# The last two chunks' routing dealt one and two steps later, with a norm, the last scaled values and the copy of turned weights moved

## The chip, the cores and the metric

The kernel runs on one core of a Trainium2 chip. The metric is the time of one execution on the device in microseconds (us), the median of several runs. A core has five engines with an instruction queue each: TensorE (PE in the profile), VectorE (DVE), ScalarE (ACT), GpSimd (POOL), and SyncE (SP), which issues most of the transfers here. An instruction waits for its semaphores at the head of its engine's queue, so that everything behind it on that engine waits too.

## The reference

The input is 32 sequences of 256 tokens with 128 features. The part that matters, shortened:

```python
h = layernorm(x) * (1 + ca) + sa
x = x + ga * attention(h)          # 16 heads of 64; softmax over the QUERY axis
h = layernorm(x) * (1 + cb) + sb
x = x + gb * moe(h)

# moe(h): 32 experts in 4 groups, 2 groups kept for each token, 6 experts of those
scores = sigmoid(h @ gate_weight.T); sc = scores + gate_bias
group_scores = top_k(sc.reshape(T, 4, 8), 2)[0].sum(-1)     # the 2 best groups are kept
topidx = top_k(where(kept, sc, -inf), 6)                    # the 6 best experts
tw = scores[topidx] / sum * 0.2
routed = sum over those experts of tw * (silu(h @ w_gate) * (h @ w_up)) @ w_down
shared = silu(h @ shared_w_gate) * (h @ shared_w_up) @ shared_w_down
anchor = one expert of 16, picked by topidx[:, 0], with weight 0.1
return routed + shared + 0.1 * anchor
```

## The kernel before

**Stages.** The tokens are cut into 16 chunks of 512. The attention stage has 128 steps (8 for each chunk, each with two heads of two sequences), numbered s, and three more in which the pipeline runs empty (to s = 130). Then come 7 steps (131 to 137) of the shared expert, each for a pair of chunks. Then come 35 lists of up to 512 gathered rows, all of one group of experts. A list j has five units k = 0 to 4, written (j, k) here.

**A step of attention.** `score_products(s)` on PE, `lowest` on DVE and `exponential` on ACT make the exponentials with their sums. `inverse_sums(s - 1)` (L568, DVE) and `scaled_values(s - 1)` (L579, POOL) divide the values by those sums into the tile `vs`. `weighted_sums(s - 2)` (L597, PE, tile `pav`) needs `vs`, and `project` (L479, tile `po`) follows.

**Portions.** The norms before and after attention and the routing are cut into portions. A table gives for each the step, relative to the first of its chunk, and the place in the step (TOP, PROD, MID, END); `deal(s, where)` issues them there. The order on each engine is the order of the program's text. From step 138 on a step is two units of a list, with TOP and PROD behind the products of the first of them and MID and END behind those of the second:

```python
if step <= last:
    half = (j * (KU + 1) + k) % 2
    for where in ((TOP, PROD), (MID, END))[half]:
        deal(step, where)
    step += half
```

The portions that matter here, for chunk c: `norm2_normalize` (L359 to L384, POOL, at 14 END), `norm2_modulate` (L394, POOL, 15 END), `norm2_send` (SP, 16 END: to DRAM and back in another order, tiles `hd_ln` and `hb_ln`), `norm2_turn` (L664, DVE, 19 TOP), `route_logits` (L479, tile `pl`, PE, and L685 `th`, ACT, 19 PROD), `route_mask` (23 TOP), `route_counts` (L762, POOL, tile `cnt`, 23 END), `route_top` (L814 and L815, memsets on POOL, then L817 to L819 on DVE, 23 MID), `route_ranks` (L479, tile `pr`, PE, 24 PROD), `route_weights` (25 TOP), `route_place` (L791 to L803, DVE, with L802, tile `to`, on POOL, 26 TOP), `route_write` (26 END) and eight `route_send` (L865, POOL, tile `rows`, 27 to 30 END). Chunk 14 begins with step 112 and chunk 15 with step 120, so that their routing falls into the shared pairs and the first lists.

**A unit of a list.** `up(j, k)` issues the products `pg` and `pu` (L1252, PE), the silu (L1256, ACT) and two products on DVE, with `pu` (L1257) and with the spread weights `bt` (L1258). Then `down` of the unit before follows (L1280, PE, tile `py`). With the first unit of list j comes `send(j - 1)`: ACT copies `py` to `y` (L1288), and POOL issues four indirect transfers of `y` to DRAM (L1291). At k = 0 SP issues the loads of the rows of list j + 3 and of the weights of list j + 2. At k = 2 `weights_turn(j + 2)` transposes the routing weights on PE (L1220, tile `pc`), copies them on ACT (L1222, tile `cwt`) and sends them to DRAM (L1224, tile `cd`); at k = 4 `weights_spread(j + 2)` loads them, repeated over the partitions (L1234, tile `bt`). At k = 1 and 3 `split_weights` (L1203 and L1207, ACT) rearranges the weights of list j + 1, and at k = 3 `rows_turn` (L1242, DVE) turns its rows.

Of the kernel before, what the change touches and what calls it, by code (L numbers as in the profile page):

```python
# [29 lines left out]
NCH = B * S // CH  # L30
# [10 lines left out]
LISTS = 2 * B * S // CH + NG - 1  # L41
# [17 lines left out]
def adaln_block_kernel(  # L59
# [23 lines left out]
    nc = tc.nc  # L83
# [155 lines left out]
    with tc.tile_pool(name="mod", bufs=1) as mp, tc.tile_pool(  # L239
# [13 lines left out]
        for b in range(BPC):  # L253
            nc.tensor.matmul(
                pmb[:, b].rearrange("p j d -> p (j d)"), silb[:, b, :], wmod_sb[:, 0 : 2 * D],
                start=True, stop=True,
# [70 lines left out]
    NS = NCH * NP  # L327
# [3 lines left out]
    with ExitStack() as actx:  # L331
# [241 lines left out]
        def scaled_values(s):  # L573
            c, t = divmod(s, NP)
            vt, rc = step_of["v", s // HALF], step_of.pop(("rc", s))
            vs = vsp.tile([P, BPC * 2, 2, DH], F32, tag="vs", name=f"vs_{s}")
            col = (t % HALF) * P
            for b in range(BPC):
                nc.gpsimd.tensor_tensor(  # L579
                    vs[:, 2 * b : 2 * b + 2],  # L580
                    vt[:, 2 * b : 2 * b + 2, col : col + P].rearrange(
                        "p k (h d) -> p k h d", h=2
                    ),
                    rc[:, b].unsqueeze(3).to_broadcast([P, 2, 2, DH]),
                    ALU.mult,
                )
            step_of["vs", s] = vs
# [295 lines left out]
        TOP, PROD, MID, END = range(4)  # L883
# [188 lines left out]

        portions = {}

        soon = {-6: 0, -5: 0, -4: 0, -3: 0, -2: 1, -1: 1, 0: 2, 1: 2}
        for c in range(NCH):
            for at, where, portion in table[0 if c else NORM1 :]:
                if c == 1 and portion is load_x:
                    continue
                if c == 1:  # L1080
                    at = soon.get(at + NP, at + NP) - NP
                portions.setdefault(c * NP + at, []).append((where, portion, c))

        def deal(s, where):
            for w, portion, c in portions.get(s, []):
                if w == where:
                    portion(c)
# [71 lines left out]
        T = [{} for _ in range(LISTS)]  # L1159
# [53 lines left out]
        def weights_turn(j):  # L1213

            t = T[j]
            rw = t.pop("rw")
            t["ix"] = mp.tile([P, NT], U32, tag="ix", name=f"iy_{j}", bufs=5)
            nc.vector.tensor_copy(t["ix"], rw[:, :, GW - 1])
            pc = ps_mm.tile([NT * OWN, P], F32, tag="mm", name=f"pc_{j}")
            nc.tensor.transpose(pc, rw.rearrange("p i w -> p (i w)"), ident)  # L1220
            cwt = mp.tile([NT * OWN, P], F32, tag="cwt", name=f"cwt_{j}", bufs=2)
            nc.scalar.copy(cwt, pc)  # L1222
            cd = cwd.tile([OWN, CH], F32, tag="cd", name=f"cd_{j}")
            nc.sync.dma_start(out=cd.rearrange("w (i p) -> i w p", p=P), in_=cwt)  # L1224
            t["cd"] = cd

        def weights_spread(j):

            t = T[j]
            cd = t.pop("cd")  # L1230
            bt = bcp.tile([P, 2, CH], F32, tag="bt", name=f"bt_{j}")
            for n, part in enumerate((cd[0:EPG], cd[EPG : GW - 1])):
                of = part.shape[0]
                nc.sync.dma_start(  # L1234
                    out=bt[:, n, :], in_=part.unsqueeze(0).to_broadcast([P // of, of, CH])
                )
            t["bt"] = bt

        def rows_turn(j):
            t = T[j]  # L1240
            t["h"] = mp.tile([P, CH], F32, tag="h", name=f"h_{j}", bufs=2)
            nc.vector.transpose(t["h"], t.pop("rh").rearrange("p x r -> p (x r)"))  # L1242
# [61 lines left out]
        def shared_up(n):  # L1304
            cs = 2 * n, 2 * n + 1
            pg, pu = (ps_sc.tile([P, CH], F32, tag="sc", name=f"{k}_{n}") for k in ("sg", "su"))
            for ps, w in ((pg, sg_sb), (pu, su_sb)):
                for h, c in enumerate(cs):
                    nc.tensor.matmul(  # L1309
                        ps[h * SI : (h + 1) * SI], w, h2_all[c], start=True, stop=True  # L1310
                    )
            a = hid.tile([P, CH], F32, tag="a", name=f"sa_{n}")
            nc.scalar.activation(a, pg, AF.Silu)
            nc.vector.tensor_mul(a, a, pu)  # L1314
            return n, a

        def shared_down(n, a, banks):
            cs = 2 * n, 2 * n + 1
            py = [
                p.tile([P, NT, D], F32, tag=tag, name=f"sy_{c}")  # L1320
                for c, (p, tag) in zip(cs, banks)
            ]
            for i in range(NT):
                for h in range(2):
                    nc.tensor.matmul(  # L1325
                        py[h][:, i, :],
                        a[h * SI : (h + 1) * SI, i * P : (i + 1) * P],
                        sd_sb[h * SI : (h + 1) * SI],
                        start=True,
                        stop=True,  # L1330
                    )
            for h, c in enumerate(cs):
                if n < PAIRS:
                    (nc.scalar.copy, nc.vector.tensor_copy)[h](
                        h2_all[c], py[h].rearrange("p i d -> p (i d)")
                    )
                    continue

                o = h2_all[c].rearrange("p (i d) -> p i d", d=D)
                for b in range(BPC):  # L1340
                    nc.vector.tensor_tensor(
                        tokens(o)[:, b], tokens(py[h])[:, b], by_batch(S_[c]["gate"])[:, b],
                        ALU.mult,
                    )
                nc.vector.tensor_add(x1_all[c], x1_all[c], o)
# [55 lines left out]
        for n in range(PAIRS):  # L1401
            now = shared_up(n)
            if prev is not None:
                shared_down(*prev, two_banks)
            prev = now
            for where in range(4):
                deal(step, where)
            step += 1
            if n == 2:
                weights_turn(0)  # L1410
            if n == 3:
                weights_turn(1)
                weights_spread(0)
            if n == 4:
                weights_spread(1)
                rows_turn(0)
            if n == 5:
                split_weights(0, "wg")
                split_weights(0, "wu")
# [10 lines left out]
        for j in range(LISTS):  # L1430

            bounds = (0, NT) if j < LISTS - 1 else (0, NT // 2, NT - 1, NT)
            parts = [slice(*p) for p in zip(bounds, bounds[1:])]
            for k, part in ((k, part) for part in parts for k in range(KU + 1)):
                a = up(j, k, part)
                if prev is not None:
                    down(*prev)
                    if prev[1] == KU:
                        send(prev[0], prev[2])
                prev = (j, k, part, a)  # L1440
                if part.start > 0:
                    continue
                if k == 0 and j + 3 < LISTS:
                    fetch_rows(j + 3)
                if k == 0 and j + 2 < LISTS:
                    fetch_weights(j + 2)
                if k == 2 and j + 2 < LISTS:
                    weights_turn(j + 2)
                if k in (1, 3) and j + 1 < LISTS:
                    split_weights(j + 1, ("wg", "wu")[k // 2])  # L1450
                if k == 3 and j + 1 < LISTS:
                    rows_turn(j + 1)
                if k == 4 and j + 2 < LISTS:
                    weights_spread(j + 2)

                if step <= last:
                    half = (j * (KU + 1) + k) % 2
# [3 lines that stand above are left out]
                elif late:  # L1461
                    late.pop(0)()

                if (j, k) in due:
                    due.pop((j, k))()
                if k == 4 and started < NCH and complete[started] <= j:
                    if started == NCH - 2:
                        load_gate(NCH - 1)
                    pass_load(started)
                    at = ((j + 2, 0), (j + 2, 4)) if j < LISTS - 2 else ((j + 1, 2), (j + 1, 4))  # L1470
                    due[at[0]] = lambda c=started: pass_sum(c)
                    due[at[1]] = lambda c=started: pass_out(c)
                    started += 1
# [62 lines left out]
```

## Time and profile before

| | |
|---|---|
| median of 3 runs | 1380.83 us (1380.76 to 1381.69) |
| the profiled execution | 1397.12 us, of which its span is 1395.2 us |
| PE busy | 1342.8 us, 96% of the span |
| DVE, ACT, POOL busy | 73%, 62%, 54% |
| mean granted clock of PE | 0.99 of full speed |
| transfers | 153.32 MB, 110 GB/s in the mean |

The profile shows one execution, which is 16.3 us longer than the median of the timed runs. The view of windows gives the busy time of each engine in stretches of the span, with the granted PE clock; 20.00 under PE in a stretch of 20 us means no pause. In the timeline a row has the start, the duration, engine, line, operation and tiles, and in brackets the idle time of that engine before it with what ended it.

### The profile page before, as it was taken

The page shows a single profiled execution, that of the slowest core. Times are in us where ns is not written, and L with a number is a line of the kernel's source. Part 1 is how long each engine was busy: PE and PEld are TensorE (multiplying, and loading weights), DVE is VectorE, ACT ScalarE, POOL GpSimd, SP SyncE. Part 2 cuts the span into 40 slices and gives each one's busy share as a digit, 9 for nine tenths or more (in the row PEclk, how much of TensorE's full clock was granted, in tenths as well). Part 3 has the DMA queues.
Part 4 walks back from the last instruction along what each step waited for, and adds up shares of the span by engine and source line. Part 5 has one row for each costly group of instructions (what it writes and reads, how often), then busy time and mean ns, then how long its engine had stood idle before and what let it go on. Part 6 is the DMA issues. An engine that isn't in the chain of part 4 may idle for free. (4 is left out here: it accounts for less than half of the span.)

```text
span 1395.2 us, 33821 instructions
## 1 busy us (share of the span) xinstructions
PE 1342.8 (96%) x10443; PEld 833.9 (60%) x10443; DVE 1024.7 (73%) x4266; ACT 868.0 (62%) x2883; POOL 758.9 (54%) x1290
## 2 busy tenths in 40 slices
PE   6999999999999999999999998889999999999995
PEld 2566566666666666556666665455566666666664
DVE  5666788778778778887887776755855557888776
ACT  3778677777777777677777776434444444454442
POOL 2536368668668668668668457444333233344342
PEclk9999999999999999999999999999999999999998
DMA  4765721221221221221221211554545557677752
GB/s 155 259 211 176 247 64 42 59 70 40 60 70 39 60 70 37 62 65 38 67 65 38 51 35 52 131 146 120 132 130 138 134 137 191 191 201 192 194 155 74
DMA packets 270686, 153.32 MB, mean 110 GB/s; under 512 B 171014, under 2 KB 234759, under 8 KB 270508
## 3 DMA queue, kind: packets, MB, share of 16 engines
q1 hardware_dynamic: 258908, 129.70, 34.9%
q0 software_dynamic: 10624, 20.40, 4.1%
q8 instruction: 85, 1.39, 0.4%
q10 hardware_dynamic: 976, 1.06, 0.2%
q14 instruction: 93, 0.76, 0.2%
HBM read 91.27 MB, written 60.61 MB: 109 GB/s over the span
## 5 line engine op out<-in xcount | busy, mean ns | idle before, releaser
L560 ACT ACTIVATE e<-e,mn 128x256 f32<-128x256 f32 (+1 forms) x1024 | 454.2, 446 | 203.6 <-DVE mn L550 163.0
L550 DVE CUSTOM_DVE_ANT_0 e<-psc,mask 128x256 f32<-128x256 f32 (+1 forms) x1024 | 306.8, 346 | 10.0 <-PE pav L597 3.8
L1291 POOL DMA_INDIRECT y_d<-y,iy x140 | 140.5, 1004 | 292.1 <-ACT y L1288 256.1
L579 POOL TENSOR_TENSOR vs<-v,rc 128x256 f32<-128x256 f32 x256 | 151.5, 613 | 228.0 <-DVE rc L568 221.2
L529 PEld LDWEIGHTS psc<-q,k 64*128 64x128 f32 x2048 | 166.2, 187 | 113.4 <-issue 101.6
L1257 DVE TENSOR_TENSOR a<-a,pu 128x512 f32<-128x512 f32 (+2 forms) x185 | 121.6, 657 | 139.3 <-PE pu L1252 57.3
L529 PE MATMUL psc<-q,k 64*128 64x256 f32 (+1 forms) x2048 | 202.1, 336 | 0.0
L597 PE MATMUL pav<-e,vs 128*64 128x256 f32 (+1 forms) x2048 | 195.0, 333 | 6.1 <-POOL vs L579 6.1
L1280 PEld LDWEIGHTS py<-wd_sb,a 128*128 128x128 f32 x1120 | 148.4, 193 | 78.2 <-issue 48.6
L560 ACT ACTIVATION_READ_ACCUMULATOR e<-e,mn 128x1 f32 x1024 | 193.7, 189 | 0.0
L1256 ACT ACTIVATE a<-pg 128x512 f32<-128x512 f32 (+2 forms) x185 | 106.1, 573 | 134.4 <-PE pg L1252 103.7
L1252 PE MATMUL pg<-h,wg 128*128 128x512 f32 (+2 forms) x370 | 182.1, 574 | 0.0
L1252 PE MATMUL pu<-h,wu 128*128 128x512 f32 (+2 forms) x370 | 181.3, 572 | 0.0
L479 PEld LDWEIGHTS po<-wo_sb,z 128*64 128x64 f32 x2048 | 122.4, 139 | 70.9 <-issue 69.7
L597 PEld LDWEIGHTS pav<-e,vs 128*64 128x64 f32 x2048 | 126.9, 136 | 58.9 <-POOL vs L579 6.8
L1280 PE MATMUL py<-wd_sb,a 128*128 x1120 | 151.7, 278 | 9.1 <-DVE a L1258 8.6
L490 DVE TENSOR_TENSOR v<-pv,bv_sb 128x512 f32<-128x512 f32 x128 | 88.4, 691 | 92.7 <-PE pv L479 66.7
L865 POOL DMA_INDIRECT rows_d<-rows,ix x128 | 130.9, 1023 | 37.5 <-issue 34.8
L500 DVE TENSOR_SCALAR q<-pq,negbq 128x512 f32<-128x512 f32 x128 | 96.0, 750 | 65.9 <-PE pq L479 64.3
L479 PE MATMUL pv<-wqkv_sb,n_t 128*64 128x512 f32 x512 | 133.1, 600 | 2.9 <-DVE q L500 2.1
L479 PE MATMUL po<-wo_sb,z 128*64 128x128 f32 x2048 | 135.2, 275 | 0.0
L479 PE MATMUL pq<-n_t,wqkv_sb 128*64 128x512 f32 x512 | 133.9, 601 | 0.7 <-ACT n_t L313 0.7
(239 smaller groups left out, 1829.3 us busy)
## 6 DMA issues: line engine op xcount, KB each, us to landing
rows_d<-blank SPq DMA_DIRECT2D x69, 366.0 KB
bt<-cd SPq DMA_DIRECT2D x70, 256.0 KB
rh<-rows_d SPq DMA_DIRECT2D x140, 64.0 KB
wgr<-in_w_gate_dram SPq DMA_DIRECT2D x35, 256.0 KB
wur<-in_w_up_dram SPq DMA_DIRECT2D x35, 256.0 KB
mb<-mod_dram SPq DMA_DIRECT2D x31, 256.0 KB
hb_ln<-hd_ln SPq DMA_DIRECT2D x124, 64.0 KB
s<-y_d SPq DMA_DIRECT2D x30, 256.0 KB
```

The source lines that it names most:

```text
L479: nc.tensor.matmul(ps[r], a[:, r], b, start=start, stop=stop)
L529: nc.tensor.matmul(pb[h][:, cols], k[r, o + kb * P : o + (kb + 1) * P], q[r, o + kb * P : o + S], start=True, stop=True,)
L550: nc.vector.tensor_tensor_reduce(e[:, cols], ps[:, cols], mask[:, cols], 1.0, 3e38, ALU.add, ALU.min, mn[:, b, kb, h : h + 1],)
L560: nc.scalar.activation(e[:, cols], e[:, cols], AF.Exp, bias=mn[:, b, kb, h : h + 1], scale=-1.0, accum_out=sm[:, b, kb, h : h + 1],)
L579: nc.gpsimd.tensor_tensor(vs[:, 2 * b : 2 * b + 2], vt[:, 2 * b : 2 * b + 2, col : col + P].rearrange("p k (h d) -> p k h d", h=2), rc[:, ...
L597: nc.tensor.matmul(pav[h * DH : (h + 1) * DH, o + kb * P : o + S], vs[:, 2 * b + kb, h, :], e[:, 0 : 2 * P] if kb == 0 else e[:, 2 * P : 3 ...
L865: sent = nc.gpsimd.indirect_dma_start(out=rows_d[:, :], out_offset=bass.IndirectOffsetOnAxis(ap=ix[:, k, i : i + 1], axis=0), in_=rows[:, ...
L1252: nc.tensor.matmul(ps[:, cols], t[key][k], t["h"][:, cols], start=True, stop=True)
L1256: nc.scalar.activation(a[:, cols], pg[:, cols], AF.Silu)
L1257: nc.vector.tensor_mul(a[:, cols], a[:, cols], pu[:, cols])
L1280: nc.tensor.matmul(t["py"][:, i, :], a[:, i * P : (i + 1) * P], w, start=k == 0 and i == part.start, stop=k == KU and i == part.stop - 1,)
L1291: sent = nc.gpsimd.indirect_dma_start(out=y_d[:, :], out_offset=bass.IndirectOffsetOnAxis(ap=ix[:, i : i + 1], axis=0), in_=y[:, i, :], in ...
```

## The change

- `scaled_values` of the last step (127) runs on DVE; the others stay on POOL.
- `norm2_normalize` of chunk 14 moves from END of step 126 to PROD of step 127, so behind `scaled_values(126)` in POOL's queue.
- The portions of chunk 14 from `route_logits` on (relative step 19 and later) come one step later, those of chunk 15 two steps later. `norm2_turn` stays where it was.
- `weights_turn` keeps the transpose on PE and the cast on DVE; the copy on ACT and the transfer to DRAM are now `weights_store`. In the lists it is issued at k = 3 and no longer at k = 2. `weights_spread` moves from k = 4 of list j to k = 1 of list j + 1. For lists 0 and 1 turning and storing stay together.

```diff
             for b in range(BPC):
-                nc.gpsimd.tensor_tensor(
+                (nc.vector if s == NS - 1 else nc.gpsimd).tensor_tensor(
                     vs[:, 2 * b : 2 * b + 2],
...
         portions = {}
 
+        late_ = {
+            NCH - 2: {norm2_normalize: (15, PROD)},
+            NCH - 1: {},
+        }
+        late_by = {NCH - 2: (19, 1), NCH - 1: (19, 2)}
+
+        def placed(c, at, where, portion):
+            if portion in late_.get(c, {}):
+                return late_[c][portion]
+            start, by = late_by.get(c, (0, 0))
+            return at + (by if at >= start and portion is not norm2_turn else 0), where
+
...
                     at = soon.get(at + NP, at + NP) - NP
+                at, where = placed(c, at, where, portion)
                 portions.setdefault(c * NP + at, []).append((where, portion, c))
...
             nc.tensor.transpose(pc, rw.rearrange("p i w -> p (i w)"), ident)
+            t["pc"] = pc
+
+        def weights_store(j):
+            t = T[j]
+            pc = t.pop("pc")
             cwt = mp.tile([NT * OWN, P], F32, tag="cwt", name=f"cwt_{j}", bufs=2)
             nc.scalar.copy(cwt, pc)
             cd = cwd.tile([OWN, CH], F32, tag="cd", name=f"cd_{j}")
...
             if n == 2:
                 weights_turn(0)
+                weights_store(0)
             if n == 3:
                 weights_turn(1)
+                weights_store(1)
                 weights_spread(0)
...
-                if k == 4 and j + 2 < LISTS:
-                    weights_spread(j + 2)
+                if k == 3 and j + 2 < LISTS:
+                    weights_store(j + 2)
+                if k == 1 and 1 <= j < LISTS - 1:
+                    weights_spread(j + 1)
```

## The prediction, made before the changed kernel ran

> **What bounds the kernel now.** First the page, for the bounding engine:
>
> ```profile
> span 1395.2 us, 33821 instructions
> ...
> PE 1342.8 (96%) x10443; PEld 833.9 (60%) x10443; DVE 1024.7 (73%) x4266; ACT 868.0 (62%) x2883; POOL 758.9 (54%) x1290
> ```
>
> PE works 96% of the span, so a change pays only where PE pauses or runs at a lower clock. Next the windows, in stretches of 20 us, to find where that is (columns: length, busy PE, PEld, DVE, ACT, POOL, then PE clock, DMA share, GB/s):
>
> ```profile
> 860.00:880.00 20.00, 13.91 (x134) 8.58 (x132) 6.69 (x33) 4.09 (x10) 15.05 (x24) 0.91 0.40 93
> ...
> 940.00:960.00 20.00, 17.91 (x80) 10.94 (x79) 12.20 (x45) 8.01 (x15) 7.40 (x17) 0.91 0.38 97
> ...
> 1000.00:1020.00 20.00, 20.00 (x97) 13.03 (x96) 13.73 (x28) 9.49 (x17) 6.05 (x6) 1.00 0.46 127
> ```
>
> From 1000 us on the lists leave PE no pause (20.00 of 20.00; a unit takes 2.61 us there, a list 13.16 us). The portions that are moved lie between the last steps of attention (856 us) and list 4 (1000 us). Finer windows:
>
> ```profile
> 856.00:1000.00 144.00, 123.03 (x705) 74.46 (x702) 89.98 (x295) 59.00 (x116) 68.86 (x110) 0.96 0.50 124
> ...
> 943.80:947.10 3.30, 3.30 (x11) 2.25 (x10) 1.24 (x2) 1.86 (x3) 0.00 (x0) 0.50 0.62 159
> ```
>
> PE is busy 123.03 of 144.00 us, so 21.0 us are idle, and the second line shows a stretch at half speed. There are three of these in this region (from 865.3, 930.1 and 943.8 us, 3.4 us each), and each loses half its length, 1.7 us. Half speed counts as busy, so the whole loss is 21.0 + 5.1 us. The timeline of PE names the pauses:
>
> ```profile
> 859.01 1.52 PE L597 MATMUL pav<-e,vs 128*64 128x256 f32 x16 [2.25 <-POOL vs L579]
> ...
> 864.22 1.86 PE L597 MATMUL pav<-e,vs 128*64 128x256 f32 x16 [2.19 <-POOL vs L579]
> ...
> 873.39 0.66 PE L479 MATMUL pl<-gw_sb,h 128*64 128x32 f32 x16 [2.52 <-issue]
> ...
> 907.30 0.66 PE L479 MATMUL pl<-gw_sb,h 128*64 128x32 f32 x16 [1.36 <-DVE h L664]
> ...
> 930.00 2.00 PE L1280 MATMUL py<-wd_sb,a 128*128 x8 [4.29 <-DVE a L1258]
> ...
> 942.49 0.30 PE L479 MATMUL pr<-cnt,ones 128*64 128x20 f32 x4 [1.73 <-POOL cnt L762]
> ...
> 949.81 1.02 PE L1252 MATMUL pg<-h,wg 128*128 128x512 f32 x2
> ...
> 960.23 1.16 PE L1280 MATMUL py<-wd_sb,a 128*128 x8 [0.60 <-DVE a L1258]
> ```
>
> The bracket is the pause ahead of the row. The first two wait for POOL's scaled values, the next two for the turned rows of chunks 14 and 15, `pr` for POOL's `cnt`, the last for a product on DVE. 949.81 is the start of unit (3,0), my clock for a list below. Of POOL, DVE and ACT in lists 2 and 3:
>
> ```profile
> 936.33 0.97 POOL L1291 DMA_INDIRECT y_d<-y,iy  x1 [9.46 <-ACT y L1288]
> ...
> 941.33 1.10 POOL L762 TENSOR_TENSOR cnt<-cnt,gm 128x4 f32<-128x4 f32 x4
> ...
> 953.49 1.03 POOL L1291 DMA_INDIRECT y_d<-y,iy  x1 [10.03 <-ACT y L1288]
> ...
> 957.37 0.98 POOL L1291 DMA_INDIRECT y_d<-y,iy  x1 [0.30 <-issue]
> ...
> 958.42 0.23 POOL L802 TENSOR_SCALAR to<-row_of 128x4 f32<-128x4 f32 x1
> ```
>
> ```profile
> 941.38 0.19 DVE L818 COPY m<-m 128x24 f32<-128x24 f32 x1 [2.32 <-POOL m L814]
> ...
> 958.68 0.19 DVE L803 SCALAR_TENSOR_TENSOR rows<-at,to 128x16 f32<-128x16 f32 x1 [1.88 <-POOL to L802]
> ```
>
> ```profile
> 952.62 0.59 ACT L1288 COPY y<-py 128x512 f32<-128x512 f32 x1 [1.15 <-PE py L1280]
> ```
>
> What matters here is a burst. In each list ACT copies the last `py` (952.62) and then POOL issues four transfers of `y`, 1.28 us apart (953.49 to 957.37 and its end at 958.35). Whatever POOL is given behind them waits: `cnt` began at 941.33 only after the four, `to` at 958.42 only after the next four. A DVE instruction that needs POOL stands just as long (2.32 and 1.88 us), and PE behind both (1.73 and 0.60 us). With T the start of `pg` of (j,0): copy at T+2.81, sends T+3.68 to T+8.54, `to` done T+8.84.
>
> **The change part by part.**
>
> *Scaled values of step 127 on DVE, norm of chunk 14 behind step 126.* Removed: the four L384 instructions and their fellows (POOL, 854.49 to 858.3, 3.8 us) from before `vs` of step 126. That `vs` can start when its inverse sums are there, 856.9, and is done at 858.1 instead of 859.5; the pause of 2.25 falls to about 0.75 (gain 1.4 to 1.5). But the norm then ends at 861.9; the memsets and `cnt` of chunk 13, which stood at 859.61 (1.03 us), end at 863.15. PE's `pr` of chunk 13 stands directly behind `pav` of step 126, so PE waits there from 859.0 to 863.15, 4.2 us where it had 0.2. DVE waits for the memset to 862.1, then has the top search of chunk 13 (0.9) and the inverse sums of step 127 to do ahead of the moved `vs`. No row shows `vs` on DVE. The nearest is L639 on DVE, two products of 128x256 in 0.72 us; the same work on POOL takes 1.18. I take 0.72 (ends 0.7 and 1.2), so it is done at 863.9 and `pav` of step 127 starts at 864.4, against 864.22 before. The pause of 2.19 is gone, but it has moved ahead of `pr`. Sum **+0.2**; ends -2.5 (if `pr` needn't wait) and +1.
>
> *What this delays.* `norm2_modulate` of 14 ends at 866.1 rather than 863.6, so `norm2_send` on SP and every load behind it on SP's queue is 2.45 us later. In the pairs the turn of chunk 14 (DVE, L664 at 872.63) is not moved, and its data now land at 874.4. `route_logits` moves behind the pair's products, so the pause of 2.52 at 873.39 is gone; but the DVE instruction behind the turn in the queue adds the last attention output and frees the bank that the next `sy` needs. It ends at 875.9 where PE would be ready at 872.5: a pause of 3.4 for one of 2.52 plus the product. Net **+0.7**; ends 0 and +2.5. The later loads on SP are covered: the first `bt` would land at 895.7 and is needed at about 896. If that cover fails it costs up to 2 us, in the range.
>
> *Logits of chunk 15 one list further on.* `pl` at 907.30 waits 1.36 us for the turned rows. Two steps later they have long been there: **-1.36**. The DVE work of `route_place` of 14, which now meets the turn, is 1.36 us in a unit of 2.61 with 1.2 us to spare: 0.
>
> *Top, counts and ranks of chunk 15.* Moved: two memsets and `cnt` on POOL, the search on DVE, `pr` on PE. They were at (2,1) and (2,2); the order after has the memsets and `cnt` at (3,0), directly behind the four sends of list 2, and `pr` at (3,1). `pr` thus comes a unit nearer to the burst than before. `cnt` ends at T+9.8 (sends end T+8.54, memsets, 1.03 of `cnt`), PE gets to `pr` at T+5.2: a pause of 4.6 where there was one of 1.73, **+2.85**. DVE stands 5 us at L818 instead of 2.32, and behind it stand the products of (3,1), whose `py` would be wanted at T+6.9; they are done soon after T+11 and lie in the same pause. The eight `rows` sends come two steps later too, between the bursts of lists 3 and 4; their list is wanted much later, 0.
>
> *Placing of chunk 15.* L802 `to` (POOL) and L803 (DVE) move from (3,1) to (4,0), again directly behind the burst. L803 runs at T+8.87; behind it on DVE stand the two products of (4,1) (0.66 us each), done T+10.4, where `py` of (4,1) is wanted at T+6.94. Pause 3.45 instead of the 0.60 at 960.23: **+2.85**.
>
> *Store of turned weights a unit later.* Per list one ACT copy of 0.26 us (L1222, 9.1 us over 35), one transfer of `cwt` and one of `bt` on SP move; none is added. At k = 3 ACT has then a silu (0.6), a split (1.5) and the copy: 2.36 of 2.61 us. `bt` comes about 7 us later, its reader at least 10 us later. On SP `bt` no longer stands behind its own `cd` (2 to 3 us) but behind the loads of rows and weights of k = 0. From list 4 on PE never pauses, and this stays so: **0**. If the cover goes, each list loses up to 1 us, 30 in all; I leave that to the last rival.
>
> *The clock.* In the trace the pause of 1.73 at 942.49 was followed by a stretch at 0.50 (943.8 to 947.1); that of 2.52 at 873.39 was not, nor that of 1.43 at 977.70. The Trainium skill, "TensorE: Matmul & The Clock Gate", section "HAM oscillation", puts the danger at PE pauses above about 3.4 us. By that rule the pause before was free and the new ones of 4.6 and 3.45 both cost a half-speed window: +3.4. By the row one of the two places had its window already, so only the second is new: +1.7. The trace decides; for the pause of 3.4 in the pairs I add half a window, 0.8: **+2.5**.
>
> Sum: 0.2 + 0.7 - 1.36 + 2.85 + 2.85 + 2.5 = +7.7, less 0.4 for `pr` of chunk 14, which now lies inside a pause of the pairs: **+7.3 us**. It is made against the profiled execution (1397.12), which is 16.3 us longer than the median; I see no part of that in the terms used except at 930.00 (below), and put the sum on the median: 1380.8 + 7.3 = 1388.1.
>
> **The rivals.**
>
> *The copy's hold is real (faster).* At 930.00 PE waited 4.29 us behind a stretch in which ACT stood before the copy L1222; 79.4 us idle stand ahead of the 35 copies. If timed runs have it too, the later copy gives back 4.29, the 1.7 of its half speed and perhaps 1.4 at 977.70, -7.4; with the gains at the end of attention (-2.5), in the pairs (-1.3) and at 907.30 (-1.4) coming through as well and the bursts costing +7.4, that is -5: 1376. Against it: records are thin in that stretch on all engines, and the profile is 16.3 us too long, so the hold may belong to the profiling; and in later lists the copy waits without any pause of PE.
>
> *The two sides cancel (within 0.2%).* The gains at the end of attention come through (-2.5), the later portions find the burst half over (+1.5 each, no new half speed): with the other terms -0.6, 1380.2.
>
> *More half speed and a late `bt` (slower still).* Three new windows (+5), or SP's loads 2.45 us later meeting the first lists (+2): +13, 1394.
>
> *The burst decides; the other side of my forecast.* It turns on one place: if POOL's sends come early enough for `cnt` at (3,0) to end before T+6.9, both terms of 2.85 and the half-speed window behind (4,0) fall away, -7.4, and the whole is 1380.7. POOL would have to begin them 2.9 us sooner, but the copy at T+2.81 fixes the start.
>
> **How the numbers follow.** The bursts at full price: 0.62. More loss: 0.13. Cancelling: 0.13. Faster through the copy: 0.12. Two tenths of a per cent (2.8 us) is what a measurement of this kernel can tell from no change. So faster 0.12, same 0.13, slower 0.75. The likeliest case alone spans 1384.5 to 1392 (the ends above). The range takes in cancelling below and the greater part of the loss above: 1379.5 to 1394.5.
>
> **What would show it.** Right: in the profile after, `pr` of chunk 15 in unit (3,1) with 4 to 5 us before it, ended by `cnt`; `py` of (4,1) with about 3.4 us, ended by the product on DVE; DVE L818 waiting about 5 us; `pr` of chunk 13 with about 4 us near 859; no pauses before `pl`; 20.00 of 20.00 from list 5 on. Wrong: these rows under 2 us; a shorter end of attention (unit (0,0) over 2 us earlier); PE pauses in the steady lists, which I price at nothing; or a time below 1378.

## The result, and the profile after

The changed kernel takes 1390.95 us (median of 4 runs, 1389.02 to 1392.99), the kernel before 1380.8 in the same comparison. The ratio is 1.0074, with an interval of 1.0055 to 1.0092: slower by 0.74%, about 10 us. The forecast was 1388.1, in a range of 1379.5 to 1394.5.

The profiled execution of the changed kernel took 1389.67 us, close to its median. That of before, on which the prediction rests, was 16 us longer than its median. A second profile of the kernel before (1378.33 us) is therefore the one compared here. First the page of the changed kernel, then that of this second profile:

```profile
span 1387.5 us, 33799 instructions
...
PE 1341.3 (97%) x10443; PEld 835.1 (60%) x10443; DVE 1027.4 (74%) x4268; ACT 865.9 (62%) x2883; POOL 760.0 (55%) x1288
```

```profile
span 1376.4 us, 33821 instructions
...
PE 1336.4 (97%) x10443; PEld 831.8 (60%) x10443; DVE 1024.7 (74%) x4266; ACT 869.5 (63%) x2883; POOL 762.1 (55%) x1290
```

The span is 11.1 us longer: 6.2 us of it are idle time of PE, and 4.9 us are its busy time, in which half speed counts. The share of 97% is the same in both and tells nothing.

Windows of the changed kernel (columns as before):

```profile
940.00:960.00 20.00, 16.32 (x66) 10.28 (x67) 10.90 (x42) 5.76 (x11) 4.12 (x10) 0.83 0.32 77
...
960.00:980.00 20.00, 16.69 (x81) 10.62 (x80) 9.86 (x17) 7.65 (x14) 11.65 (x14) 1.00 0.50 132
...
1000.00:1020.00 20.00, 19.95 (x96) 12.52 (x95) 14.57 (x28) 9.61 (x17) 7.13 (x8) 1.00 0.59 142
...
943.60:950.10 6.50, 6.42 (x22) 4.25 (x23) 3.25 (x20) 0.77 (x2) 0.23 (x2) 0.50 0.05 17
```

Lists 3 and 4 hold 3.7 and 3.3 us of pause in two stretches of 20 us, and one long stretch at half speed, 6.5 us of which are cut out in the last line. From 1000 to 1020 us PE works 19.95 of 20.00. The lines of the changed kernel's lists have numbers higher by 19 (L1310 is L1291 of before, L1299 is L1280, L1277 is L1258), and L1344 is L1325. PE's timeline of the changed kernel, the rows with long pauses:

```profile
857.49 0.30 PE L479 MATMUL pr<-cnt,ones 128*64 128x20 f32 x4 [3.28 <-POOL rows L659]
...
870.90 1.33 PE L1344 MATMUL sy<-sd_sb,sa 64*128 64x128 f32 x14 [3.17 <-issue]
...
943.68 0.41 PE L479 MATMUL pr<-cnt,ones 128*64 128x20 f32 x4 [4.33 <-POOL cnt L762]
...
965.59 1.16 PE L1299 MATMUL py<-wd_sb,a 128*128 x8 [3.31 <-DVE a L1277]
```

For the kernel before, its second profile has these in their place:

```profile
864.44 0.66 PE L479 MATMUL pl<-gw_sb,h 128*64 128x32 f32 x16 [2.52 <-DVE h L664]
...
897.25 0.66 PE L479 MATMUL pl<-gw_sb,h 128*64 128x32 f32 x16 [1.36 <-DVE h L664]
...
926.14 0.30 PE L479 MATMUL pr<-cnt,ones 128*64 128x20 f32 x4 [1.72 <-POOL cnt L762]
...
943.90 1.16 PE L1280 MATMUL py<-wd_sb,a 128*128 x8 [0.59 <-DVE a L1258]
```

The pauses before `pl` (2.52 and 1.36) are gone. In their place stand 3.28 before `pr` of chunk 13, 3.17 before `sy`, 4.33 before `pr` of chunk 15 where there were 1.72, and 3.31 before `py` of (4,1) where there were 0.59. POOL's timeline of the changed kernel shows what stands ahead of the last two:

```profile
937.65 0.97 POOL L1310 DMA_INDIRECT y_d<-y,iy  x1 [4.63 <-ACT y L1307]
...
941.47 0.97 POOL L1310 DMA_INDIRECT y_d<-y,iy  x1 [0.30 <-issue]
...
942.58 1.05 POOL L762 TENSOR_TENSOR cnt<-cnt,gm 128x4 f32<-128x4 f32 x4
...
962.72 0.97 POOL L1310 DMA_INDIRECT y_d<-y,iy  x1 [0.30 <-issue]
...
963.78 0.23 POOL L802 TENSOR_SCALAR to<-row_of 128x4 f32<-128x4 f32 x1
```

The four sends of `y` begin at 937.65; the last one begins at 941.47, and `cnt` follows at 942.58, behind two short memsets, ends at 943.63, and `pr` starts at 943.68. A list later `to` begins at 963.78, right behind the last send. VectorE stands at the head of its queue for the same thing:

```profile
942.62 0.22 DVE L818 COPY m<-m 128x24 f32<-128x24 f32 x1 [4.63 <-POOL m L814]
...
964.03 0.18 DVE L803 SCALAR_TENSOR_TENSOR rows<-at,to 128x16 f32<-128x16 f32 x1 [4.60 <-POOL to L802]
```

It idles 4.63 us for the memset and 4.60 us for `to`, and the products `a` that PE wants are issued behind these.

Where the time went is best read from a common point, since up to step 124 the instructions are the same and yet the starts of that step differ by up to 4 us (842.1 to 846.4). In this table (worked out from the starts of instructions in the traces, in us) the first `pav` of step 124 is zero; the 51st `pg` lies at the start of list 5. The kernels from p_end on are the experiments of the next section.

| kernel | pav of step 127 | 51st pg | end of span |
|---|---|---|---|
| before, second profile | 13.30 | 118.57 | 534.33 |
| changed | 14.13 | 126.81 | 542.43 |
| p_end | 14.57 | 120.91 | 536.33 |
| p_late14 | 13.28 | 124.40 | 540.05 |
| p_late15 | 13.31 | 124.34 | 539.64 |
| p_store | 13.30 | 120.05 | 535.41 |
| x_15by1 | 13.55 | 120.09 | 536.05 |
| x_pool | 14.59 | 117.37 | 532.70 |
| b_15by1 | 13.30 | 112.86 | 528.50 |
| x_turn14 | 14.60 | 125.60 | 541.23 |
| best_a | 10.93 | 113.95 | 529.64 |
| best_b | 10.15 | 111.79 | 527.75 |
| best_c | 10.15 | 116.50 | 532.13 |

The change costs 8.1 us here: 0.8 at the end of attention, 0.7 more by the first `pg` of the lists (46.34 against 47.83), 6.75 in lists 0 to 4, and nothing in the thirty lists behind (415.76 us from the 51st `pg` to the end against 415.62). The second profile of before, p_store, p_late15 and b_15by1 have the same order up to the first `pg`, and reach it at 46.3, 46.4, 44.8 and 44.8: half-speed stretches fall differently from one execution to the next. So a single row is good to about 1.5 us. The 6.75 us of the lists stand clear of that, the 0.8 and 0.7 by themselves do not.

### The profile page after: what moved, and what is told of

Its sections match the earlier page's. It is cut to its first block, busy times and chain, and to the rows that moved or that the text cites. A ratio compares the mean times of both kernels' runs of the same rounds, so it can differ in the third digit from the quotient of the medians.

```text
span 1387.5 us, 33799 instructions
## 1 busy us (share of the span) xinstructions
PE 1341.3 (97%) x10443; PEld 835.1 (60%) x10443; DVE 1027.4 (74%) x4268; ACT 865.9 (62%) x2883; POOL 760.0 (55%) x1288
## 5 line engine op out<-in xcount | busy, mean ns | idle before, releaser
L1310 POOL DMA_INDIRECT y_d<-y,iy x140 | 139.9, 999 | 291.6 <-ACT y L1307 253.8
L1299 PEld LDWEIGHTS py<-wd_sb,a 128*128 128x128 f32 x1120 | 147.8, 193 | 73.6 <-issue 52.8
L1299 PE MATMUL py<-wd_sb,a 128*128 x1120 | 151.2, 277 | 4.8 <-DVE a L1277 4.6
```

The costliest lines, as they stand in the source:

```text
L1299: nc.tensor.matmul(t["py"][:, i, :], a[:, i * P : (i + 1) * P], w, start=k == 0 and i == part.start, stop=k == KU and i == part.stop - 1,)
L1310: sent = nc.gpsimd.indirect_dma_start(out=y_d[:, :], out_offset=bass.IndirectOffsetOnAxis(ap=ix[:, i : i + 1], axis=0), in_=y[:, i, :], in ...
```

## The experiments

The ratios are to the kernel before, with their intervals.

**A second profile of the kernel before (b_again).** No edit.

> The kernel before, unchanged, for a second profile. If the hold of ACT at 920 to 926 us and the pause of 4.29 us at 930.00 belong to that one profiled execution, they are not here, and the span is about 1379 us; if they belong to the kernel, they are.

1378.33 us. ACT's hold and the pause of 4.29 us are not there. Nor is there such a pause in p_end, p_late14, p_late15, b_15by1, best_a or best_c, all of which keep the copy at k = 2. They belonged to that one execution, and the rival built on them falls.

**Each part alone.** These four are the kernel before with one part of the change each. In the code of the changed kernel p_end is

```diff
-        late_by = {NCH - 2: (19, 1), NCH - 1: (19, 2)}
+        late_by = {NCH - 2: (19, 0), NCH - 1: (19, 0)}
...
                 if k == 2 and j + 2 < LISTS:
                     weights_turn(j + 2)
+                    weights_store(j + 2)
...
-                if k == 3 and j + 2 < LISTS:
-                    weights_store(j + 2)
-                if k == 1 and 1 <= j < LISTS - 1:
-                    weights_spread(j + 1)
+                if k == 4 and j + 2 < LISTS:
+                    weights_spread(j + 2)
```

> The kernel before with the end of attention alone changed: norm of chunk 14 behind the scaled values of step 126, and those of step 127 on VectorE. My theory: +0.4 us up to the last weighted sums, and the rows of chunk 14 arrive 2.4 us later, while the logits that wait for them stay where they were, so their pause of 2.5 us grows to about 5: +2.5 to +3 us in all (ratio 1.002). Rival (the gains come through): -2.5 us, ratio 0.998.

Ratio 1.0020 (1.0011 to 1.0029), 1383.17 against 1380.46 us: +2.7, the size that was expected. PE's timeline of p_end:

```profile
854.65 0.41 PE L479 MATMUL pr<-cnt,ones 128*64 128x20 f32 x4 [3.28 <-POOL rows L659]
...
866.95 0.82 PE L479 MATMUL pl<-gw_sb,h 128*64 128x32 f32 x16 [3.40 <-DVE h L664]
```

A pause of 3.28 us before `pr` of chunk 13 has come in. The one before `pl` of chunk 14 has 3.40 us for 2.52, less than the 5 expected, and the last `pav` came 1.3 us later (14.57 for 13.30) where 0.4 was expected. The length of this pause is no good measure, though. In p_store, whose order is that of before here, it is 3.96 us:

```profile
866.09 1.06 PE L479 MATMUL pl<-gw_sb,h 128*64 128x32 f32 x16 [3.96 <-DVE h L664]
```

Counted from the zero of the table, `pl` starts at 22.34 us both there and in the second profile of before, and at 24.68 in p_end. The logits come 2.3 us later, as expected (2.4); how much of that PE spends waiting depends on when it gets there.

The row that I had mis-sized stands in VectorE's timeline of the changed kernel, and POOL's has a second one beside it:

```profile
857.66 1.66 DVE L579 TENSOR_TENSOR vs<-v,rc 128x256 f32<-128x256 f32 x2
```

```profile
857.44 1.59 POOL L394 TENSOR_TENSOR ln_xh<-ln_xh,mb 128x256 f32<-128x256 f32 x2
```

The two products with the inverse sums take 1.66 us on VectorE here. POOL does the same in 1.18, and my estimate was 0.72. But 1.66 is not what VectorE needs for them. In best_b and best_c, further down, POOL has another row beside them, and they take half as long. VectorE's and POOL's timelines of best_c:

```profile
851.76 0.89 DVE L579 TENSOR_TENSOR vs<-v,rc 128x256 f32<-128x256 f32 x2
```

```profile
851.69 2.17 POOL L384 TENSOR_SCALAR ln_xh<-x,ln_out,ln_nm 128x128 f32<-128x128 f32 x4
```

All six profiles with L394 beside the products have 1.65 or 1.66 us, both with L384 have 0.88 or 0.89. So the price goes with POOL's work at that moment; which property of the two rows does it was not tried.

p_late14 undoes everything but the delay of chunk 14; the copy and the spreading are put back as above.

```diff
-            NCH - 2: {norm2_normalize: (15, PROD)},
+            NCH - 2: {},
...
-        late_by = {NCH - 2: (19, 1), NCH - 1: (19, 2)}
+        late_by = {NCH - 2: (19, 1), NCH - 1: (19, 0)}
...
-                (nc.vector if s == NS - 1 else nc.gpsimd).tensor_tensor(
+                nc.gpsimd.tensor_tensor(
```

> The kernel before with chunk 14's routing one step later alone. My theory: the pause of 2.5 us before its logits goes, and a pause of about 1.5 us before the shared product sy takes its place, as the bank is freed behind the turn on DVE: -1 us (-2 to 0; ratio 0.999). Rival: the later sends of its rows meet the first burst of y on POOL, +2 us (ratio 1.0015).

Ratio 1.0044 (1.0031 to 1.0057), about +6 us. This expectation was wrong in sign. What it said of the pairs came: no row waits before `pl` of chunk 14, `sy` waits 1.53 us, and the first `pg` stands 42.7 us behind the zero instead of 46.3. Lists 0 to 4 lose 9.4 us. In PE's timeline of p_late14 one row has the greater part of that, and POOL's shows why:

```profile
934.50 0.41 PE L479 MATMUL pr<-cnt,ones 128*64 128x20 f32 x4 [6.84 <-POOL cnt L762]
```

```profile
916.17 0.97 POOL L1310 DMA_INDIRECT y_d<-y,iy  x1 [0.30 <-issue]
...
917.44 1.14 POOL L865 DMA_INDIRECT rows_d<-rows,ix  x1 [0.30 <-issue]
...
925.68 0.97 POOL L865 DMA_INDIRECT rows_d<-rows,ix  x1 [0.30 <-issue]
...
926.96 0.97 POOL L1310 DMA_INDIRECT y_d<-y,iy  x1 [0.30 <-issue]
...
930.78 0.97 POOL L1310 DMA_INDIRECT y_d<-y,iy  x1 [0.30 <-issue]
...
932.18 0.97 POOL L865 DMA_INDIRECT rows_d<-rows,ix  x1 [0.16 <-issue]
...
933.17 1.27 POOL L762 TENSOR_TENSOR cnt<-cnt,gm 128x4 f32<-128x4 f32 x4
```

Seven sends of rows of chunk 14 (917.44 to 925.68 are the first and the last) now stand between the sends of list 0 and list 1; the four of list 1 are late for that (926.96 to 930.78), the eighth of the rows follows, and only then `cnt` of chunk 15, at 933.17. PE waits 6.84 us where it waited 1.72, and two half-speed units lie there (930.8 to about 938, the first of them within the pause) where one did. The pause before `pl` of chunk 15 is longer too, 2.73 us for 1.36. The rival had the mechanism, the meeting with a burst of `y`, but not its size: the sends delay the burst and the burst delays `cnt`, which in this kernel is not late.

p_late15 is the same with chunk 15 alone late.

```diff
-        late_by = {NCH - 2: (19, 1), NCH - 1: (19, 0)}
+        late_by = {NCH - 2: (19, 0), NCH - 1: (19, 2)}
```

> The kernel before with chunk 15's routing two steps later alone. My theory (POOL's four sends of y stand ahead of cnt and of to): +2.85 and +2.85 us for the two pauses, +1.7 for one more half-speed window, -1.4 for the logits of chunk 15: +6 us (ratio 1.0043), with pauses of 4 to 5 us before pr at (3,1) and 3 to 3.5 us before py of (4,1). Rival (the bursts are covered): -1 us.

Ratio 1.0036 (1.0023 to 1.0049), +5 us; +5.3 in the table. PE's timeline of p_late15:

```profile
940.97 0.30 PE L479 MATMUL pr<-cnt,ones 128*64 128x20 f32 x4 [4.33 <-POOL cnt L762]
...
961.46 1.57 PE L1299 MATMUL py<-wd_sb,a 128*128 x8 [3.31 <-DVE a L1277]
```

The pauses are those of the changed kernel to the hundredth, 4.33 and 3.31, and no row waits before `pl` of chunk 15. So the two pauses need nothing else of the change.

p_store keeps only the later copy and spreading, with both chunks at 0 in `late_by`.

> The kernel before with the copy of turned weights at k = 3 and their spreading at k = 1 of the next list alone. My theory: 0 us (within 1; ratio 1.000), PE without pauses from list 5 on. Rival (the copy held ACT in timed runs too): -6 us (ratio 0.9957). Rival (the later bt or the fuller ACT at k = 3 shows): +3 us or more, with pauses of PE before py in every list.

Ratio 0.9999 (0.9988 to 1.0010). The later copy neither gains nor costs.

The parts alone add up to 2.7 + 6 + 5 + 0 = 14 us, the whole costs 10. The wait that p_late14 adds before `cnt` of chunk 15 is not there once chunk 15 is late too.

**Where the bursts are missed.** x_15by1 is the changed kernel with chunk 15 one step late.

```diff
-        late_by = {NCH - 2: (19, 1), NCH - 1: (19, 2)}
+        late_by = {NCH - 2: (19, 1), NCH - 1: (19, 1)}
```

> The changed kernel with chunk 15's routing one step later and not two, so that memsets, cnt and pr come at (2,3) and (2,4) and the placing at (3,3), half a list behind the burst of y. My theory: the pauses of 4.3 and 3.3 us go, and one half-speed window with them, -7 to -9 us against the changed kernel: about +1 us against before (-1 to +3; ratio 1.000 to 1.002). Rival (the time lies elsewhere in the change, the delay itself or the sends of rows): still +7 us or more (ratio 1.005).

Ratio 1.0017 (1.0005 to 1.0028), +2.3 us. One constant takes most of the loss away. PE's timeline of x_15by1:

```profile
868.41 2.04 PE L1344 MATMUL sy<-sd_sb,sa 64*128 64x128 f32 x14 [4.74 <-issue]
...
934.27 0.30 PE L479 MATMUL pr<-cnt,ones 128*64 128x20 f32 x4 [1.62 <-POOL cnt L762]
```

Before `pr` 1.62 us are left, because the rows of chunk 14 come late here as in p_late14. The pause before `py` is gone. The one before `sy` is longer than in the changed kernel (4.74).

x_pool keeps the order of the changed kernel and takes the work off POOL.

```diff
-            nc.gpsimd.memset(m6, FILL)
-            nc.gpsimd.memset(m1, FILL)
+            (nc.vector if c == NCH - 1 else nc.gpsimd).memset(m6, FILL)
+            (nc.vector if c == NCH - 1 else nc.gpsimd).memset(m1, FILL)
...
-                nc.gpsimd.tensor_tensor(cnt[:, i + 1, :], ...)
+                (nc.vector if c == NCH - 1 else nc.gpsimd).tensor_tensor(cnt[:, i + 1, :], ...)
...
-            nc.gpsimd.tensor_scalar_add(to, row_of, float(c * CH))
+            (nc.vector if c == NCH - 1 else nc.gpsimd).tensor_scalar_add(to, row_of, float(c * CH))
```

> The changed kernel with the order kept, but chunk 15's two memsets, the four cnt additions and to on VectorE in place of POOL, so that none of them stands behind the four sends of y. My theory: the pauses before pr at (3,1) and before py of (4,1) fall under 1 us each and no half-speed window follows: -7 to -9 us against the changed kernel, +1 to +3 against before (ratio 1.001 to 1.002). Rival (these pauses come from a fuller VectorE): they stay, and 1 us of VectorE work is added, ratio 1.007 or more.

Ratio 0.9986 (0.9973 to 0.9998), 1379.32 against 1381.88 us. Windows of x_pool:

```profile
900.00:960.00 60.00, 60.00 (x295) 38.06 (x294) 43.94 (x127) 28.48 (x52) 27.64 (x32) 1.00 0.58 147
...
960.00:1000.00 40.00, 39.95 (x184) 24.68 (x183) 30.98 (x69) 18.95 (x33) 18.46 (x19) 1.00 0.58 151
```

PE has no pause in 60 us of lists 0 to 4 and 0.05 us in the next 40. Seven small instructions moved to another queue, at the same place in the order, take off more than the whole change cost. In the table that is 9.7 us less than the changed kernel (7 to 9 were expected). It ends below the kernel before, where +1 to +3 was expected: lists 0 to 4 take 68.2 us here and 72.2 in the second profile of before, whose pauses there, 1.36, 1.72 and 0.59, and the half speed behind the second of them are gone as well. The fuller VectorE is refuted as a cause.

b_15by1 is the kernel before with chunk 15 one step late, and nothing else; against p_late15 it is

```diff
-        late_by = {NCH - 2: (19, 0), NCH - 1: (19, 2)}
+        late_by = {NCH - 2: (19, 0), NCH - 1: (19, 1)}
```

> The kernel before with chunk 15's routing one step later alone. My theory: the pauses of 1.73 us before pr and 0.60 before py go, the half-speed window behind the first too (1.7), and the logits' 1.36 falls: -4 to -5 us (ratio 0.9965). Rival (the sends of rows then meet a burst instead): -1 us or more than that.

Ratio 0.9957 (0.9948 to 0.9967), 1375.98 us: -5.9. Windows of b_15by1:

```profile
900.00:960.00 60.00, 60.00 (x297) 38.33 (x295) 42.08 (x113) 28.90 (x51) 28.51 (x38) 1.00 0.60 157
...
960.00:1000.00 40.00, 39.65 (x183) 24.59 (x182) 30.32 (x70) 19.28 (x33) 15.85 (x16) 1.00 0.55 144
```

With one step `cnt` comes in the middle of a list, behind a burst that is over (it begins at 928.68, the last send at 926.75), and PE waits for nothing there. `to` still follows a burst directly (941.56 behind a send at 940.51), but half a list on, where PE does not wait for it. With two steps, as with none, PE arrives before POOL has done.

**The shared pairs.** x_turn14 is the changed kernel with the turn of chunk 14 late too.

```diff
-            return at + (by if at >= start and portion is not norm2_turn else 0), where
+            return at + (by if at >= start and (portion is not norm2_turn or c == NCH - 2) else 0), where
```

> The changed kernel with the turn of chunk 14 moved one step later as well, so that it stands behind the last attention output on VectorE and not ahead of it. My theory (the output, which frees the bank for sy, waits behind the turn): the pause of 3.17 us before sy goes, and at times a half-speed window with it: -3 to -5 us against the changed kernel, +5 to +7 against before (ratio 1.004 to 1.005). Rival (sy waits for something else, or the logits now wait as long for the turn): -1 to 0, ratio 1.0065 or more.

Ratio 1.0051 (1.0037 to 1.0065). That is 3 us under the changed kernel's, but the two intervals overlap and the table gives 1.2, so a gain in time is not shown. PE's timeline of x_turn14:

```profile
868.67 0.73 PE L479 MATMUL pl<-gw_sb,h 128*64 128x32 f32 x16 [1.49 <-DVE h L664]
```

The pause of 3.17 before `sy` is gone, which bears out that the bank was held behind the turn; 1.49 us have come back before `pl`.

**Can the end of attention gain?** Three kernels take its pauses away in different ways; all have chunk 15 one step late. best_a is b_15by1 with the scaled values of step 127 on VectorE:

```diff
-                nc.gpsimd.tensor_tensor(
+                (nc.vector if s == NS - 1 else nc.gpsimd).tensor_tensor(
```

best_c has besides the norm of chunk 14 behind step 126, and the edit of x_pool for chunk 13 as well:

```diff
-            NCH - 2: {},
+            NCH - 2: {norm2_normalize: (15, PROD)},
...
-            nc.gpsimd.memset(m6, FILL)
+            (nc.vector if c in (NCH - 3, NCH - 1) else nc.gpsimd).memset(m6, FILL)
```

and so on for the memset of `m1`, `cnt` and `to`. best_b is best_c with chunk 14 one step late, its turn included as in x_turn14, and with the later copy.

> The kernel before with chunk 15's routing one step later and the scaled values of step 127 on VectorE; the norm of chunk 14 stays where it was. My theory: b_15by1 (ratio 0.9957) and -1 to -2 us more, as the pause of 2.19 us before the last pav falls to about 0.5: ratio 0.9945. Rival (VectorE's 1.66 us for the two products and its wait for POOL's memset use that up): 0.9957.

> The changed kernel with chunk 15 one step later, the turn of chunk 14 late with its logits, and memsets, cnt and to of chunks 13 and 15 on VectorE. My theory: the pause before pr of chunk 13 (3.3 us) and the one before sy (3 to 4.7) go, with those of lists 3 and 4 gone already, and fewer half-speed windows follow: -6 to -11 us against before (ratio 0.992 to 0.9955). Rival (the pauses move on to the next late operation): within 3 us of before.

> The kernel before with chunk 15 one step later, the end of attention as in the changed kernel, and memsets, cnt and to of chunks 13 and 15 on VectorE; chunk 14's routing is not late. My theory: 3 us are gained at the end of attention (no pause before pr of chunk 13), and some 2 of them are lost to the logits of chunk 14, whose turned rows come no sooner: -5 to -8 us (ratio 0.995). Rival: as the end of attention alone (p_end), 2.7 us worse than b_15by1: ratio 0.9975.

best_a: 0.9977 (0.9966 to 0.9987). best_b: 0.9960 (0.9946 to 0.9974), 1374.47 us, the lowest median of all. best_c: 0.9977 (0.9968 to 0.9986). All three reach the last `pav` 2.4 to 3.2 us sooner than before, yet none is shown to be better than b_15by1 (0.9957), and best_c ends behind it, by 3.6 us in the table and with intervals that do not meet; best_a does so by 1.1 us in the table, less than a row is good to, and the two intervals just overlap. None gained what was expected of it; best_c has the ratio that its rival named (0.9975). PE's timelines of best_a, best_c and best_b:

```profile
868.37 1.07 PE L479 MATMUL pl<-gw_sb,h 128*64 128x32 f32 x16 [6.07 <-DVE h L664]
```

```profile
866.01 1.07 PE L479 MATMUL pl<-gw_sb,h 128*64 128x32 f32 x16 [8.58 <-DVE h L664]
```

```profile
868.90 1.07 PE L479 MATMUL pl<-gw_sb,h 128*64 128x32 f32 x16 [4.49 <-DVE h L664]
```

What was gained stands before `pl` of chunk 14 again: 6.07, 8.58 and 4.49 us for 2.52. In the traces the turn of chunk 14 starts 21.6 us after the zero of the table in the second profile of before, and 21.4, 23.0 and 22.9 in these three. In these three it waits for data that go through DRAM, as VectorE's row of best_c shows, and PE's speed ahead of it doesn't bring them sooner:

```profile
865.24 0.71 DVE L664 STREAM_TRANSPOSE h<-hb_ln 128x512 f32<-128x512 f32 x1 [5.64 <-DMA hb_ln<-hd_ln]
```

Behind the longer pause the clock is low for longer. In b_15by1 one stretch of 3.4 us between the last `pav` and the logits is at half speed, where PE has to wait anyway. In best_a it is about 10 us, from 864.4 on, and some 6 us of them lie behind the start of `pl` (868.37). From `pl` to the first `pg` best_a takes 25.4 us and b_15by1 22.4; half of 6 us is that difference. Part of it is made up later, as b_15by1 has a half-speed stretch at the start of the lists (891.6) that best_a has not. So the account fits, but it was not tried by itself. A window of best_a:

```profile
864.40:873.60 9.20, 5.23 (x30) 2.39 (x32) 1.93 (x4) 0.87 (x2) 6.82 (x8) 0.50 0.65 136
```

## Why the prediction was right

It was right in sign, in size and, at most steps, in place: the two long pauses in the lists stand where it put them, ended by what it named, and x_pool takes both away. By its steps:

- **Scaled values and norm: +0.2 was forecast, +0.8 measured** (13.30 to 14.13). The pause before `pr` of chunk 13 is there (3.28, forecast 4.2), and the one before step 127 is gone. The mis-sized term is the two products on VectorE, 1.66 us for 0.72 and outside the ends of 0.7 and 1.2. L639 was the wrong row to price them by: it reads `po`, which lies in PSUM, where the moved products read SBUF alone. What was left out is that the products would run beside L394 of the norm on POOL; beside L384 they take 0.88.
- **Shared pairs: +0.3 forecast (0.7 less 0.4 for `pr` of chunk 14), +0.7 measured,** which the scatter of 1.5 us does not tell apart. The turn of chunk 14 came 2.75 us later (forecast 2.45), and `sy` waited 3.17 us (3.4).
- **Logits of chunk 15: the pause of 1.36 is gone**, as forecast.
- **Top, counts and ranks: +2.85 forecast.** The pause went from 1.72 to 4.33, so +2.6, ended by `cnt`; L818 waited 4.63 us (forecast 5).
- **Placing: +2.85 forecast.** From 0.59 to 3.31, so +2.7, ended by the product behind L803.
- **Clock: 1.5 more half-speed windows were forecast, one in the lists and half of one in the pairs; two more are in the profiles**, five against three between 843 and 1000 us. Behind the two new pauses the count is as forecast, one more than before, but not the places: two follow the pause of 4.33 (943.6 to 950.1 at 0.50) and none the one of 3.31, while in p_late15 one follows each. The rule of the Trainium skill (TensorE: Matmul & The Clock Gate, "HAM oscillation"), pauses above about 3.4 us, is no sharp limit here: half speed followed the pause of 1.72 in the second profile of before (the line under this list) but not the same pause in p_end, and that of 3.31 in p_late15 but not in the changed kernel. The other one lies at the start of list 0 (892.0 to 895.4), where no new pause stands; p_store, which does not have the two pauses, has one there too.
- **Store and spreading: 0 forecast, a ratio of 0.9999 measured.** The same from list 5 to the end.

The window of the second profile of before that the row on the clock speaks of:

```profile
927.00:930.00 3.00, 3.00 (x6) 1.25 (x5) 0.37 (x5) 1.72 (x3) 0.10 (x1) 0.50 0.57 136
```

Logits, the two pauses and the window in the lists came to 6.04 us in the prediction, and lists 0 to 4 took 6.75 more. In all, 7.3 was forecast, 8.1 is in the profiles, and the timed ratio gives 10, with an interval of 7.6 to 12.7. The four timed runs have mean clocks of 0.989, 0.989, 0.987 and 0.990, and the last is that of the slowest (1392.99 us), so more half speed does not explain that run. Whether the last 2 us are anything but chance stays open.

The rival that the copy's hold was real fell with the second profile; that of cancelling fell with p_end and p_late15. The rival on the other side named the right point: with `cnt` and `to` off POOL (x_pool) both terms disappear. What the prediction didn't see is that its parts were not independent. The sends of rows of chunk 14 had no term in it; chunk 14's delay alone (p_late14) gains in the pairs and yet costs 6 us in all. In the changed kernel these sends stand in POOL's queue just as long (917.34 to 932.87), and only because chunk 15 is late as well does `cnt` not wait behind them. That the sum came out without this term is luck.

## What to carry to other kernels

A portion moved by a whole step keeps its work but changes what is ahead of it in each queue: find the periodic bursts of the engine that it uses (here four sends of 1.28 us in every list), and place it between them, or take its few small instructions to another queue. Price a delayed transfer by what it pushes in turn, not alone; the parts of such a change don't add up. Price an instruction that moves to another engine with the neighbour that it will run beside, not by a row from elsewhere. And before a pause is taken away, ask whether what comes behind it waits for data with a time of their own: then the pause only moves.

## What the runs showed of the hardware

Two products of 128x256 in fp32 with the broadcast inverse sums, both inputs in SBUF, took 1.18 us on POOL. On VectorE they took 1.65 or 1.66 us in the six profiles where POOL ran `norm2_modulate` (L394, two products of 128x256) beside them, and 0.88 or 0.89 in the two where it ran the four L384. POOL's rows are longer beside them too: L394 has 1.59 us in the changed kernel and 1.41 in best_c, where it runs later, and L384 has 2.17 in best_c and 1.74 in the changed kernel, where it runs earlier.

An indirect transfer keeps POOL's queue for about 1.28 us (0.97 and a gap of 0.30), so four of them hold back what stands behind them by some 5 us.

Half-speed stretches come in units of some 3.4 us that don't line up with the pause: the pauses of 4.33 and 3.31 us (3.32 in x_turn14) were followed by two units and none in the changed kernel, and by one each in p_late15 and x_turn14. Pauses of 6.07 us (best_a) and 8.58 us (best_c) lay with about 10 us at half speed, three units, of which a part falls into the pause itself.
